# Sums placed between a product's halves, and a slot's other stages moved behind the scores

## The chip, the cores and the metric

The program runs on one core of a Trainium2 chip. Its engines are TensorE (PE, with its weight loads shown as PEld), VectorE (DVE), ScalarE (ACT), GpSimd (POOL) and SyncE (SP, which issues the DMAs). Each engine works through its own queue in order and waits at semaphores for the others. The time is the device time of one execution in microseconds; lower is better. All data are 32-bit floats.

## The reference

An encoder layer runs over a short context (2 x 77 rows of 512), and a decoder layer over 2 x 2048 rows of 512 with 16 heads of 32, a causal self-attention with relative bias, a cross-attention to the encoder's output and a feed-forward part of 2048. Cut to the decoder, where nearly all of the time is:

```python
y = tgt
yn = _ln(y, dec_n1_s, dec_n1_b)
y = y + _mha(yn, yn, dec_sa_in_w, dec_sa_in_b, dec_sa_out_w, dec_sa_out_b, sb)   # causal, biased
y = y + _mha(_ln(y, dec_n2_s, dec_n2_b), memory, dec_ca_in_w, dec_ca_in_b, dec_ca_out_w, dec_ca_out_b, cb)
h = _ln(y, dec_n3_s, dec_n3_b)
y = y + (relu(h @ dec_ff1_w.T + dec_ff1_b) @ dec_ff2_w.T + dec_ff2_b)
```

`_mha` makes q, k and v, takes `softmax(q @ k.T / sqrt(32) + bias) @ v` by heads, and multiplies by the output weights.

## The kernel before

**Blocks and units.** Self-attention comes first, up to about 1640 us. The rows are cut into eight blocks of 512 (`blocks`, two batches of four, m = 0 to 3), and a block's work into 16 units (`units`: four groups g of four heads by four tiles t of 128 rows). Unit n has 4 m + t + 1 tiles of keys, taken in pieces of up to four. The loop at L1893 goes through the pieces, up to two of a unit at a time, in this order of issue: `turn` (TensorE transposes the probabilities, ACT and DVE copy them out of PSUM), then, where the unit ends, `slot(n + 1)`, then some late exponentials (`exps`, on ACT), then scores of a unit further on (`score_two` or `score_next`; TensorE at L375, DVE takes the maxima at L384 and L391), then `values` (TensorE at L456). The scores run one to two units ahead of the turn.

**Slots.** The projections and everything else that a block needs are hung on units by hand in three lists: `light`, `jobs` and `late`. `slot(n)` (L1324) runs all of `light[n]`, then the products `jobs[n]`, then `late[n]`. `light` holds the norm of the block to come (`norm_load`, `norm_stats`, `norm_center`, and `norm_turn` with four transposes on TensorE at L305 and four copies on ACT at L310), the four steps of `spread` (reciprocals of the softmax sums on DVE, their DMAs, a multiplication on POOL), the loads of bias tiles (`load_bias`), the output's residual sums on POOL (`out_done`), the sums of tokens on POOL (`token_sums`) and weight sums for later stages (`wc_sums`, `w2_sums`, `w1_sums`). `late` holds further sums, residual loads and stores. Slot u + k of a block that begins at unit u is called slot k here; slots -5 to -1 lie in the block before.

**Products.** From the second block of a batch on, q, k, v and the output projection are made by a scheme of Strassen and Winograd's kind: a product of 512 x 512 by 512 becomes seven of half the size, numbered 1 to 7 (`PARTS`), whose results are added into the quarters "11", "12", "21", "22" of the output. `part_job` (L1108) makes one such product for k, v or the output (o): four matmuls of 256 columns in the code, two for each half f of one PSUM bank, and then sums on DVE. `pair_job` (L1032) makes two products for one half of q (a or b) with two matmuls each, in the two halves of one bank, so "a16" is products 1 and 6 of half a. `last[0]` tells a product that it is the last of its slot; `part_job` then sums each half of the bank for itself (L1150), after all of its matmuls. `todo` (L1202) puts the products on slots; the output's are at slots 6 to 9 of the next block (L1223).

**PSUM.** All matmuls write into one tile `psum` of eight banks; `bank()` (L180) hands them out in a ring, so a bank is taken again eight takings later. Semaphores between the engines are drawn from what each instruction reads and writes, in the order of the code.

**Weights.** `load_next` (L1268) is called before each product and issues the weight loads of products to come on SP, into three buffers `wqk`.

Of the kernel before, what the change touches and what calls it, by code (L numbers as in the profile page):

```python
# [12 lines left out]
ALU = mybir.AluOpType  # L13
# [41 lines left out]
def tile_encoder_decoder(ctx: ExitStack, tc: tile.TileContext, ins, out):  # L55
# [103 lines left out]
    with (  # L159
# [252 lines left out]
        def turn(pieces):  # L412

            first = units[pieces[0][0]][1] == 0
            loads = []
            for n, k0, kn in pieces:
                ks = range(k0, k0 + kn)
                if first:
                    heads = [(n, k, r) for r in range(HC) for k in ks]
                    loads += [heads[o : o + TB] for o in range(0, len(heads), TB)]  # L420
                else:
                    loads += [[(n, k, r) for r in range(HC)] for k in ks]
            for o, load in enumerate(loads):
                pt = bank()
                pts = in_turn("pts", pts_all).rearrange("p (x q) -> p x q", q=P)
                for x, (n, k, r) in enumerate(load):
                    nc.tensor.transpose(pt[:, ts(x, P)], state[n]["p"][r][:, k], ident)  # L427
                    got[n, k, r] = pts[:, x, :]
                w = len(load) * P
                free = pieces[0][0] == len(units) - 2 and (pieces[0][1] or o >= 4)  # L430
                if free or (o % 2 if first else o in (4, 6) if len(loads) == 8 else o >= (len(loads) + 1) // 2):
                    nc.vector.tensor_copy(pts[:, : len(load), :], pt[:, :w])  # L432
                else:
                    nc.scalar.copy(pts[:, : len(load), :], pt[:, :w])  # L434
# [597 lines left out]
        def pair_job(b, m, h, parts):  # L1032
# [8 lines left out]
            def run(w):  # L1041
                if parts[0] == 1:
                    for g in (2 * h, 2 * h + 1):
                        qTs[b, m, g] = sb.tile([P, MB], F32, name="q", tag="q", bufs=3)
                mm = bank()
                for j, i in enumerate(parts):
                    n = of_nT(b, m, PARTS[i][1])
                    for c in range(2):
                        nc.tensor.matmul(mm[:, ts(j, TOK)], w[:, 2 * j + c, :], n[:, c, :], start=c == 0, stop=c == 1)  # L1049
# [3 lines left out]
                got = [mm[:, ts(j, TOK)] for j in range(len(parts))]  # L1053
                if parts == (1, 6):
                    ve.tensor_scalar(d["11"], got[0], qbias[:, 2 * h : 2 * h + 1], None, ALU.add)
                    ve.tensor_tensor(d["12"], got[1], d["11"], ALU.add)
                elif parts == (7, 4):
                    ve.scalar_tensor_tensor(d["22"], got[0], qstep[:, h : h + 1], d["12"], ALU.add, ALU.add)
                    ve.tensor_tensor(d["21"], got[1], d["22"], ALU.add)
                elif parts == (2, 5):  # L1060
                    for to, j in (("11", 0), ("12", 1), ("22", 1)):
                        ve.tensor_tensor(d[to], got[j], d[to], ALU.add)
                else:
                    assert parts == (3,)
                    ve.tensor_tensor(d["12"], got[0], d["12"], ALU.add)

            return load, run, True
        n_tiles, last = {}, [False]
        PARTS = {
# [3 lines left out]
        ADDS = {2: ("11",), 3: ("12",), 5: ("22", "12")}  # L1073
# [34 lines left out]
        def part_job(kind, b, m, i):  # L1108
# [20 lines left out]
            def run(w):  # L1129
                n, mm = of_o(b, m, by) if kind == "o" else of_nT(b, m, by), bank()  # L1130
                left, right = (w, n) if kind == "k" else (n, w)
                for f in range(2):
# [4 lines left out]
                got = mm.rearrange("p (f n) -> p f n", f=2)  # L1137
                d = {to: place(to) for to in ("11", "12", "21", "22")}
                if i == 1 and kind == "k":
                    for f in range(2):  # L1140
                        nc.scalar.activation(
                            d["11"][:, f, :], got[:, f, :], AF.Identity, bias=vec("dec_sa_in_b", NC + f)
                        )
                elif i == 1:
                    nc.scalar.copy(d["11"], got)
                elif last[0] and not (i == 7 and kind == "k"):
                    for f in range(2):
                        for to in {6: ("12",), 7: ("22",), 4: ("21",)}.get(i) or ADDS[i]:
                            onto = {6: "11", 7: "12", 4: "22"}.get(i, to)
                            ve.tensor_tensor(d[to][:, f, :], got[:, f, :], d[onto][:, f, :], ALU.add)  # L1150
                elif i == 6:
                    ve.tensor_tensor(d["12"], got, d["11"], ALU.add)
                elif i == 7 and kind == "k":
                    for f in range(2):
                        ve.scalar_tensor_tensor(
                            d["22"][:, f, :], got[:, f, :], kstep[:, f : f + 1], d["12"][:, f, :], ALU.add, ALU.add
                        )
                elif i == 7:
                    ve.tensor_tensor(d["22"], got, d["12"], ALU.add)
                elif i == 4:  # L1160
                    ve.tensor_tensor(d["21"], got, d["22"], ALU.add)
                else:
                    for to in ADDS[i]:
                        ve.tensor_tensor(d[to], got, d[to], ALU.add)
# [20 lines left out]
        late = {n: [] for n in light}  # L1185

        for x, (b, m) in enumerate(blocks):
# [13 lines left out]
            else:  # L1201
                todo = {  # L1202
                    -5: "a16 a74", -4: "k1 k6", -3: "k7 k4", -2: "k2 a25", -1: "k5 k3 a3", 0: "v1 v6", 1: "v7 v4 v2",
                    2: "v5 v3", 3: "b16", 4: "b74 b25", 5: "b3",
                } if x % NMB > 1 else {
                    -4: "k1 a16 k6", -3: "a74 k7", -2: "k4 k2 a25", -1: "k5 k3 a3", 0: "v1 v6", 1: "v7 v4 v2",
                    2: "v5 v3", 3: "b16", 4: "b74 b25", 5: "b3",
# [116 lines left out]
        def slot(n):  # L1324
            for f in light[n]:
                f()
            for k, (_, run, _) in enumerate(jobs[n]):
# [3 lines left out]
                ran[0] += 1  # L1331
            for f in late[n]:
                f()
# [132 lines left out]
        for c, k in enumerate((0, 2, 4, 10)):  # L1466
            light[u + k + 2].append(lambda c=c: w2_store(c, 1))
# [425 lines left out]
        while i < len(stream):  # L1893
# [7 lines left out]
            turn(pair)  # L1901
# [7 lines left out]
            if ends and n + 1 < end:  # L1909
# [84 lines left out]
```

## Time and profile before

| what | value |
|---|---|
| median of 3 runs | 2726.84 us (2726.21 to 2733.03) |
| profiled execution: time | 2728.59 us |
| profiled execution: span, first to last instruction | 2726.8 us |
| granted TensorE clock, mean | 0.997 |
| self-attention, from the first turn to the last one's begin | 27.6 to 1641.3 us |
| cross-attention and feed-forward | 1641.3 to 2726.8 us |

The profile gives, for each group of instructions, its line, engine and operation, the tile that it writes and those that it reads, the shapes, the count, then the busy time in us and the mean of one in ns, and behind the second bar the idle time of the engine just before, with what ended it. A matmul of the code that takes 32-bit floats appears as two records. In the timeline the columns are start and length in us, then the instruction, the count of like ones merged into the row, and in brackets the idle time before it and its releaser. The ends of matmuls are modelled, so starts are the safer measure.

### The profile page before, as it was taken

Reading aid. Unit: us, or ns where it says so; the run is one execution under the profiler, and the core shown is the slowest. Engines: PE = TensorE matmul, PEld = TensorE weight load, DVE = VectorE, ACT = ScalarE, POOL = GpSimd, SP = SyncE. Lnnn points to the kernel's source line nnn. Section 1 sums busy time; section 2 is a strip of 40 time slices with the busy share of each in tenths; the row PEclk is TensorE's granted clock in tenths of the full one; section 3 lists DMA queues with packets and bytes.
Section 4 is the critical chain, followed back from the end, with each engine's and each line's share of the span. In section 5 each row is a group of like instructions: output and inputs, shape, how many; then the busy total and the mean of one; then the engine's idle time right before and its main releaser. Section 6 shows DMA issues by size and latency. Waiting matters only on the chain.

```text
span 2726.8 us, 68267 instructions
## 1 busy us (share of the span) xinstructions
PE 2708.1 (99%) x26606; PEld 2217.9 (81%) x26606; DVE 1839.9 (67%) x5445; ACT 1537.0 (56%) x2978; POOL 1002.4 (37%) x844
## 2 busy tenths in 40 slices
PE   9999999999999999999999999999999999999998
PEld 6678877777876677777777777898989898989898
DVE  4776688888885677788888783646464746464645
ACT  3554567777786547667777784444444444444431
POOL 2612235500300513322300203455556565656456
PEclk9999999999999999999999999999999999999999
DMA  8724355511213522343311206565657565656465
GB/s 242 213 92 135 126 155 164 168 50 43 67 45 89 143 76 72 111 133 98 126 50 35 79 19 220 171 214 173 213 171 239 168 216 170 218 166 219 151 224 185
DMA packets 296277, 385.10 MB, mean 141 GB/s; under 512 B 41184, under 2 KB 165648, under 8 KB 295826
## 3 DMA queue, kind: packets, MB, share of 16 engines
q1 hardware_dynamic: 295954, 380.73, 44.1%
q8 instruction: 211, 3.46, 0.5%
q14 instruction: 112, 0.92, 0.1%
HBM read 334.15 MB, written 46.47 MB: 140 GB/s over the span
## 4 chain that ended last, share of the span: by engine, by line
PE 95%; DVE 1%; ACT 1%; DMA 1%; POOL 1%; issue 1%; SPq 0%; DVEq 0%; POOLq 0%; ACTq 0%
PE psum L427 18%; PE psum L1638 14%; PE psum L1667 13%; PE psum L375 11%; PE psum L456 9%; PE psum L1134 8%; PE psum L1801 3%; PE psum L1758 3%; PE psum L1049 3%; PE psum L866 2%; PE psum L836 1%; PE psum L874 1%; PE psum L590 1%; PE psum L811 1%; PE psum L239 1%; PE psum L215 1%
## 5 line engine op out<-in xcount | busy, mean ns | idle before, releaser
L406 ACT ACTIVATE pp<-pp,nm 128x128 f32<-128x128 f32 (+15 forms) x512 | 611.8, 1200 | 28.6 <-DVE nm L401 27.8
L384 DVE TENSOR_SCALAR_CACHE_REDUCE pp<-psum 128x512 f32<-128x512 f32 (+3 forms) x1024 | 556.2, 591 | 51.3 <-PE psum L375 49.7
L434 ACT COPY pts<-psum 128x512 f32<-128x512 f32 x714 | 384.1, 594 | 312.6 <-PE psum L427 265.6
L427 PE MATMUL psum<-ident,pp 128*128 128x128 f32 x4352 | 530.4, 277 | 4.7 <-ACT nT L310 4.0
L427 PEld LDWEIGHTS psum<-ident,pp 128*128 128x128 f32 x4352 | 474.0, 141 | 55.7 <-DVE pp L384 21.4
L375 PE MATMUL psum<-kT,q 32*128 32x512 f32 (+3 forms) x2560 | 336.5, 559 | 2.5 <-DVE q L217 1.0
L456 PEld LDWEIGHTS psum<-pts,vv 128*32 128x32 f32 x8704 | 226.4, 110 | 127.4 <-DVE pp L384 55.4
L1667 PE MATMUL psum<-pp 128*128 128x128 f32 x2560 | 304.5, 276 | 1.9 <-POOL pp L962 1.6
L1667 PEld LDWEIGHTS psum<-pp 128*128 128x128 f32 x2560 | 296.3, 192 | 8.6 <-issue 2.8
L432 DVE COPY pts<-psum 128x512 f32<-128x512 f32 x374 | 245.2, 685 | 82.6 <-PE psum L427 80.3
L456 PE MATMUL psum<-pts,vv 128*32 128x128 f32 x8704 | 279.6, 276 | 0.8 <-DVE mx L391 0.3
L962 POOL TENSOR_TENSOR pp<-pp 128x512 f32<-128x512 f32 x159 | 212.8, 1356 | 111.0 <-DMA pp<-in_dec_ff_wT_dram 50.6
L1638 PE MATMUL psum<-vv,pp 128*128 128x256 f32 x1024 | 236.2, 381 | 0.0
L375 PEld LDWEIGHTS psum<-kT,q 32*128 32x128 f32 x2560 | 146.3, 183 | 107.1 <-issue 41.3
L1638 PEld LDWEIGHTS psum<-vv,pp 128*128 128x128 f32 x1024 | 190.3, 190 | 25.8 <-issue 0.5
L391 DVE CUSTOM_DVE_ANT_0 pp<-psum,bias 128x256 f32<-128x256 f32 (+1 forms) x512 | 196.0, 411 | 19.7 <-PE psum L375 19.7
L1651 DVE TENSOR_TENSOR kT<-kT,psum 128x512 f32<-128x512 f32 x96 | 65.8, 686 | 191.6 <-PE psum L1638 191.4
L1654 ACT ACTIVATE kT<-kT,vecs 128x256 f32<-128x256 f32 x192 | 86.9, 501 | 156.6 <-DVE kT L1651 155.9
L1638 PE MATMUL psum<-nT,pp 128*128 128x256 f32 x768 | 174.1, 380 | 0.5 <-DVE oT L471 0.5
L1638 PEld LDWEIGHTS psum<-nT,pp 128*128 128x128 f32 x768 | 144.2, 190 | 20.8 <-issue 1.4
L1675 ACT COPY oT<-psum 128x128 f32<-128x128 f32 x56 | 15.0, 268 | 238.9 <-PE psum L1667 238.9
L494 POOL TENSOR_TENSOR oT<-rirows,oT 128x512 f32<-128x512 f32 x30 | 38.4, 1280 | 293.6 <-DMA rirows<-rec 181.7
(272 smaller groups left out, 4110.6 us busy)
## 6 DMA issues: line engine op xcount, KB each, us to landing
pp<-w_d SPq DMA_DIRECT2D x520, 256.0 KB
pp<-in_dec_ff_wT_dram SPq DMA_DIRECT2D x112, 256.0 KB
bias<-tzg SPq DMA_DIRECT2D x128, 128.0 KB
pp<-wo_d SPq DMA_DIRECT2D x56, 256.0 KB
wqk<-in_dec_sa_in_wT_dram SPq DMA_DIRECT2D x52, 256.0 KB
wqk<-sa_q SPq DMA_DIRECT2D x84, 128.0 KB
vv<-in_enc_ff_wT_dram SPq DMA_DIRECT2D x8, 1024.0 KB
xr<-in_x_dram SPq DMA_DIRECT2D x32, 256.0 KB
```

The lines of the kernel that those rows point to most:

```text
L375: nc.tensor.matmul(banks[r][:, : kn * P], q[rows4(r), ts(t, P)], kT[rows4(r), g, k0 * P : (k0 + kn) * P], start=True, stop=True,)
L384: nc.vector.tensor_scalar(p[:, k0 : k0 + far], s[:, :far], 1.0, None, ALU.mult, ALU.max, accum_out=st["mx"][:, r, c : c + 1],)
L391: nc.vector.tensor_tensor_reduce(p[:, k0 + far : i + 1], s[:, far:kn], near[:, 2 - (kn - far) :], 1.0, LOWEST, ALU.add, ALU.max, accum_out ...
L406: nc.scalar.activation(p, p, AF.Exp, bias=nm, accum_out=to)
L427: nc.tensor.transpose(pt[:, ts(x, P)], state[n]["p"][r][:, k], ident)
L432: nc.vector.tensor_copy(pts[:, : len(load), :], pt[:, :w])
L434: nc.scalar.copy(pts[:, : len(load), :], pt[:, :w])
L456: nc.tensor.matmul(ot[rows4(r)], vv[:, k, ts(g * HC + r, HD)], got.pop((n, k, r)), start=k == k0 and (whole or not begun), stop=k == k1 - ...
L962: engine.tensor_tensor(out, a, b, ALU.subtract)
L1134: nc.tensor.matmul(mm[:, ts(f, TOK)], left[:, c, ts(f, P)], right[:, c, :], start=c == 0, stop=c == 1,)
L1638: nc.tensor.matmul(mm[:, ts(f, TOK)], a[:, c, ts(f, P)], b[:, c, :], start=fresh and f == 0 and c == 0, stop=c == 1, skip_group_check=True,)
L1667: nc.tensor.matmul(psum[:, bank_i, ts(col, P)], lhs[:, c, :], w[:, c, :], start=fresh and k in (0, 3) and c == 0, stop=c == 3, skip_group_ ...
```

## The change

Four things change.

1. In `pair_job` each of the two products is summed as soon as its two matmuls are issued, ahead of the matmuls of the second. In `part_job` a slot's last product (all but product 1) sums the first half of its bank ahead of the second half's matmuls; k's product 7, which was summed by halves behind all matmuls, now does so only as last of its slot. Others are summed behind all matmuls, as before.
2. Pairs 25 become 52, so that product 5, which is added to two quarters, comes first; "k2 a25" becomes "a52 k2"; the output's products 2 and 5 change places. Product 5's two additions change their order.
3. In the units of the second block of a batch and later, and after units 9 and 10, only the slot's products stay behind the turn. What is in `light` and `late` is issued behind the scores, ahead of the values. One list of stores (`w2_store` of the second part) moves to a list `ahead`, which runs before the products.
4. `turn` is told whether it is followed by such a slot without products (`direct`), and then gives other copies to DVE and puts its late exponential two copies before the end.

```diff
-        def turn(pieces):
+        def turn(pieces, direct):
...
-                w = len(load) * P
+                w, half = len(load) * P, len(loads) // 2
                 free = pieces[0][0] == len(units) - 2 and (pieces[0][1] or o >= 4)
-                if free or (o % 2 if first else o in (4, 6) if len(loads) == 8 else o >= (len(loads) + 1) // 2):
+                if free or (o % 2 if first else o >= half and (len(loads) - o) % 2 if direct else o in (4, 6) if len(loads) == 8 else o >= (len(loads) + 1) // 2):
...
-                if not first and o == (7 if len(loads) == 8 else min(3, len(loads) - 1)):
+                if not first and o == (max(0, len(loads) - 2) if direct else 7 if len(loads) == 8 else min(3, len(loads) - 1)):
                     exps(1)
...
-                for j, i in enumerate(parts):
-                    n = of_nT(b, m, PARTS[i][1])
-                    for c in range(2):
-                        nc.tensor.matmul(mm[:, ts(j, TOK)], w[:, 2 * j + c, :], n[:, c, :], start=c == 0, stop=c == 1)
...
-                elif parts == (2, 5):
-                    for to, j in (("11", 0), ("12", 1), ("22", 1)):
-                        ve.tensor_tensor(d[to], got[j], d[to], ALU.add)
...
+                for j, i in enumerate(parts):
+                    n, got = of_nT(b, m, PARTS[i][1]), mm[:, ts(j, TOK)]
+                    for c in range(2):
+                        nc.tensor.matmul(got, w[:, 2 * j + c, :], n[:, c, :], start=c == 0, stop=c == 1)
+                    if i == 1:
+                        ve.tensor_scalar(d["11"], got, qbias[:, 2 * h : 2 * h + 1], None, ALU.add)
+                    elif i == 7:
+                        ve.scalar_tensor_tensor(d["22"], got, qstep[:, h : h + 1], d["12"], ALU.add, ALU.add)
+                    else:
+                        for to, onto in SUMS[i]:
+                            ve.tensor_tensor(d[to], got, d[onto], ALU.add)
...
+        SUMS = {
+            2: (("11", "11"),), 3: (("12", "12"),), 4: (("21", "22"),), 5: (("12", "12"), ("22", "22")),
+            6: (("12", "11"),), 7: (("22", "12"),),
+        }
...
+                def sums(f):
...
+                    elif i == 7 and kind == "k":
+                        for x in range(2)[f]:
+                            ve.scalar_tensor_tensor(
+                                d["22"][:, x, :], got[:, x, :], kstep[:, x : x + 1], d["12"][:, x, :], ALU.add, ALU.add
+                            )
+                    else:
+                        for to, onto in SUMS[i]:
+                            ve.tensor_tensor(d[to][:, f], got[:, f], d[onto][:, f], ALU.add)
+
+                halves = last[0] and i != 1
                 for f in range(2):
                     for c in range(2):
                         nc.tensor.matmul(
                             mm[:, ts(f, TOK)], left[:, c, ts(f, P)], right[:, c, :], start=c == 0, stop=c == 1,
                         )
...
+                    if halves:
+                        sums(slice(f, f + 1))
+                if not halves:
+                    sums(slice(0, 2))
...
-                    -5: "a16 a74", -4: "k1 k6", -3: "k7 k4", -2: "k2 a25", -1: "k5 k3 a3", 0: "v1 v6", 1: "v7 v4 v2",
-                    2: "v5 v3", 3: "b16", 4: "b74 b25", 5: "b3",
+                    -5: "a16 a74", -4: "k1 k6", -3: "k7 k4", -2: "a52 k2", -1: "k5 k3 a3", 0: "v1 v6", 1: "v7 v4 v2",
+                    2: "v5 v3", 3: "b16", 4: "b74 b52", 5: "b3",
...
-                    for k, part in ((0, 1), (0, 6), (1, 7), (1, 4), (2, 2), (2, 5), (3, 3)):
+                    for k, part in ((0, 1), (0, 6), (1, 7), (1, 4), (2, 5), (2, 2), (3, 3)):
...
+        def products(n):
+            for f in ahead[n]:
+                f()
             for k, (_, run, _) in enumerate(jobs[n]):
                 load_next()
                 last[0] = k == len(jobs[n]) - 1
                 run(loaded[ran[0]])
                 ran[0] += 1
+
+        def slot(n):
+            for f in light[n]:
+                f()
+            products(n)
             for f in late[n]:
                 f()
...
-            light[u + k + 2].append(lambda c=c: w2_store(c, 1))
+            ahead[u + k + 2].append(lambda c=c: w2_store(c, 1))
...
-            turn(pair)
+            parted = ends and n + 1 < end and (units[n][1] > 0 or n in (9, 10))
+            turn(pair, parted and not jobs[n + 1])
...
-            if ends and n + 1 < end:
+            if parted:
+                products(n + 1)
+            elif ends and n + 1 < end:
                 slot(n + 1)
...
+            if parted:
+                for f in light[n + 1] + late[n + 1]:
+                    f()
             if third and not ends:
                 exps(1)
             values(pair)
```

More of the change, by code (lines that the diff above doesn't have):

```diff
@@ L1052, in run @@
                 }
[L1053 to L1059, printed above, removed]
-                elif parts == (2, 5):
-                    for to, j in (("11", 0), ("12", 1), ("22", 1)):
[L1062 to L1065, printed above, removed]
+                for j, i in enumerate(parts):
[9 more added lines that the diff above has]
+                            ve.tensor_tensor(d[to], got, d[onto], ALU.add)
             return load, run, True
         n_tiles, last = {}, [False]
+        SUMS = {
+            2: (("11", "11"),), 3: (("12", "12"),), 4: (("21", "22"),), 5: (("12", "12"), ("22", "22")),
+            6: (("12", "11"),), 7: (("22", "12"),),
+        }
         PARTS = {
@@ L1131, in run @@
                 left, right = (w, n) if kind == "k" else (n, w)
+                got = mm.rearrange("p (f n) -> p f n", f=2)
+                d = {to: place(to) for to in ("11", "12", "21", "22")}
+                def sums(f):
+                    if i == 1 and kind == "k":
+                        for x in range(2)[f]:
+                            bi = vec("dec_sa_in_b", NC + x)
+                            nc.scalar.activation(d["11"][:, x, :], got[:, x, :], AF.Identity, bias=bi)
+                    elif i == 1:
+                        nc.scalar.copy(d["11"][:, f], got[:, f])
+                    elif i == 7 and kind == "k":
+                        for x in range(2)[f]:
+                            ve.scalar_tensor_tensor(
[5 more added lines that the diff above has]
+                halves = last[0] and i != 1
                 for f in range(2):
@@ L1136, in run @@
                         )
[L1137 to L1164, printed above, removed]
+                    if halves:
+                        sums(slice(f, f + 1))
+                if not halves:
+                    sums(slice(0, 2))
             return load, run, True
@@ L1184, in tile_encoder_decoder @@
         light = {n: [] for n in range(-1, len(units) + NU)}
-        late = {n: [] for n in light}
+        late, ahead = {n: [] for n in light}, {n: [] for n in light}
         for x, (b, m) in enumerate(blocks):
@@ L1202, in tile_encoder_decoder @@
                 todo = {
[L1203 to L1204 removed]
+                    -5: "a16 a74", -4: "k1 k6", -3: "k7 k4", -2: "a52 k2", -1: "k5 k3 a3", 0: "v1 v6", 1: "v7 v4 v2",
+                    2: "v5 v3", 3: "b16", 4: "b74 b52", 5: "b3",
                 } if x % NMB > 1 else {
[L1206 to L1207 removed]
+                    -4: "k1 a16 k6", -3: "a74 k7", -2: "k4 a52 k2", -1: "k5 k3 a3", 0: "v1 v6", 1: "v7 v4 v2",
+                    2: "v5 v3", 3: "b16", 4: "b74 b52", 5: "b3",
                 }
@@ L1323, in tile_encoder_decoder @@
         light[6].append(lambda: make_bias(2, rel, v))
-        def slot(n):
-            for f in light[n]:
+        def products(n):
+            for f in ahead[n]:
                 f()
```

1 line of the change is left out of this document (removed).

## The prediction

> **What bounds the kernel now.** I read the page first (busy shares, then the chain that ended last), then the stretches of the blocks, then one slot of the timeline, then TensorE's waits.
>
> ```profile
> span 2726.8 us, 68267 instructions
> PE 2708.1 (99%) x26606; PEld 2217.9 (81%) x26606; DVE 1839.9 (67%) x5445; ACT 1537.0 (56%) x2978; POOL 1002.4 (37%) x844
> ...
> PE 95%; DVE 1%; ACT 1%; DMA 1%; POOL 1%; issue 1%; SPq 0%; DVEq 0%; POOLq 0%; ACTq 0%
> ```
>
> TensorE is busy 99% of the span and carries 95% of the chain, so whatever delays TensorE delays the end, and what shortens another engine gains only the little that TensorE waits for it.
>
> ```profile
> 369.57:589.55 219.98, 219.88 (x2658) 171.41 (x2657) 182.38 (x625) 160.15 (x276) 84.84 (x71) 1.00 0.48 144
> ...
> 1641.31:2726.80 1085.49, 1077.72 (x8408) 975.02 (x8404) 587.66 (x1128) 434.67 (x925) 596.43 (x505) 1.00 0.60 194
> ```
>
> These are the third block of the first batch and everything after attention, which the change does not touch. Columns: length, then busy time of PE, PEld, DVE, ACT, POOL, the granted clock, the DMA. In the block DVE is busy 182.38 of 219.98 us (83%) and TensorE all of it. So all that can move lies before 1641 us, and there the other engines have room while TensorE has none.
>
> One slot of the fourth block, with the products o7 and o4 (the code's four matmuls show as eight records of a product; x16 is both):
>
> ```profile
> 702.63 3.62 PE L1134 MATMUL psum<-wqk,oT 128*128 128x256 f32 x16
> ...
> 706.17 0.74 PEld L375 LDWEIGHTS psum<-kT,q 32*128 32x128 f32 x14 [0.33 <-issue]
> 706.18 1.88 PE L375 MATMUL psum<-kT,q 32*128 32x256 f32 x16
> 706.34 0.76 DVE L1150 TENSOR_TENSOR wbig<-psum,wbig 128x256 f32<-128x256 f32 x2 [1.02 <-PE psum L1134]
> ...
> 707.15 0.29 PEld L375 LDWEIGHTS psum<-kT,q 32*128 32x128 f32 x2 [0.23 <-DVE wbig L1150]
> ```
>
> The records start (3.62 - 0.38) / 15 = 0.216 us apart (0.38 is the mean of one in the rows below). o4's last starts at 705.87 and its first half's last at 702.63 + 11 x 0.216 = 705.01. L1150 here is already split into two 256-column sums, and the first reads only the first half. It starts at 706.34, 0.47 after the last record of the whole product, though DVE had been idle since 705.32 and the first half alone would have let it start at 705.48. So a read of one half of a bank is held until what was issued before it into the other half is done: the order between engines is kept by bank, not by column. This is the row that the forecast hangs on.
>
> **The change part by part.** (1) *Sums between the halves.* The code issues the first half's matmuls, its sum, then the second half's matmuls, into the same bank. If order is kept by bank, the second half's first matmul waits for the sum. How often: six blocks take the split products, each with the pairs 16, 74, 52 for two halves a and b (6) and, as a slot's last product, k6, k4 or k7, k2, v6, v2, v3 (6): 72. The output product of seven blocks has o6, o4, o2, o3 as last ones: 28. Together 100; in 12 of them (the pairs 52) the first half is summed twice. Durations:
>
> ```profile
> L1134 PE MATMUL psum<-wqk,oT 128*128 128x256 f32 x280 | 65.3, 380 | 0.0
> ...
> L1150 DVE TENSOR_TENSOR wbig<-psum,wbig 128x256 f32<-128x256 f32 x70 | 25.8, 418 | 29.3 <-PE psum L1134 20.9 <-ACT wbig L1145 6.6 <-ACT kT L867 1.0
> ...
> L1062 DVE TENSOR_TENSOR q<-psum,q 128x256 f32<-128x256 f32 x36 | 13.0, 418 | 10.5 <-PE psum L1049 10.5
> ...
> L1055 DVE TENSOR_SCALAR q<-psum,qbias 128x256 f32<-128x256 f32 x12 | 5.8, 483 | 11.4 <-PE psum L1049 11.4
> ```
>
> One stop of TensorE: 0.47 from the half's last record to the sum's start, 0.42 for the sum, 0.05 from its end to TensorE's next (L1150 ended at 707.10, the weight load of L375 began at 707.15), less the 0.216 after which the record would have started anyway: 0.72 us. Queued behind the waiting matmul are the rest of the product, the scores and the values, all that TensorE has. Sum: 88 x 0.72 = 63.4; 12 x (0.72 + 13.0/36) = 13.0; the pairs 16 and 74 start with a longer sum (L1055 483 ns; I take the same for L1058), 24 x 0.06 = 1.4: 77.8 us.
>
> That holds where DVE is free when the half is ready, which is 4 x 0.216 = 0.86 us before the whole product is. Idle time of DVE before a product's first sum, waiting for TensorE: L1055 11.4 us over 12 products, L1062 10.5 over 12 (three sums each), 0.95 and 0.88 us, so DVE is mostly free; where it is late, one eviction is in front:
>
> ```profile
> L432 DVE COPY pts<-psum 128x512 f32<-128x512 f32 x374 | 245.2, 685 | 82.6 <-PE psum L427 80.3
> ```
>
> Bounds: 0, or half of the stops behind one eviction, 50 x 0.685 = 34 us. I take 6, near the low end, since the idle rows show DVE free.
>
> The trace shows only DVE waiting for TensorE inside one bank, not TensorE for DVE. So the stop is bounded by 0 and 77.8 us; I take the whole, because the one direction that is visible is kept by bank although columns are disjoint.
>
> [...]
>
> (2) *What the stops pay back.* While TensorE stands, DVE and ACT go on evicting, and the scores that follow find banks freer:
>
> ```profile
>   issue: 41.3, 136
>   DVE pts L432: 14.5, 64
>   ACT pts L434: 6.7, 40
>   DVE wbig L1150: 3.5, 7
>   ACT nT L310: 3.1, 6
> ...
>   DVE kT L1164: 2.1, 4
>   DVE q L1062: 2.0, 5
> ```
>
> This is the line of the scores, L375: idle time before its matmuls and weight loads (us, times) and what ended it. The waits that name an eviction or a sum are 14.5 + 6.7 + 3.5 + 2.1 + 2.0 = 28.8 us, of all slots. Bounds of the gain: 0 and 28.8; I take 16, as some of these slots have no stop, and a weight load's wait is not always TensorE's. The "issue" row waits for nothing and stays.
>
> (3) *Other stages after the scores.*
>
> ```profile
> PE psum L427 <- ACT nT L310: 4.0, 2, 2.2
> ...
> L282 DVE BATCH_NORM_STATS2 bnst<-xt 128x6 f32<-128x512 f32 x28 | 19.0, 677 | 4.5 <-DMA xt<-in_x_dram 4.5
> ...
> L482 DVE RECIPROCAL ri<-sums 128x16 f32<-128x16 f32 x30 | 7.3, 242 | 0.0
> ```
>
> DVE work such as a norm's statistics (0.68 us) or a reciprocal (0.24) leaves its place in front of the sums, and the normalised tile's four ACT evictions theirs. Gain: the waits that name nT, 4.0 at the transposes and 3.1 at the scores, 7.1 at most. Against it, the norm's transposes now take a bank that the scores have just used; in the slot above the wait for a bank was 0.23. At four a block, six blocks: 24 x 0.23 = 5.5 at most. I take 7.1 less the middle of 0 to 5.5, a gain of 4.
>
> What hides the rest of the move: the bias, residual, norm and reciprocal DMAs now stand on SP behind the weight loads, which wait long for a buffer, and POOL's token sums start later.
>
> ```profile
> SPq L1118 <- PE psum L1134: 343.1, 56, 15.8
> ...
> 506.92 1.27 POOL L962 TENSOR_TENSOR xr<-nT,xt 128x512 f32<-128x512 f32 x1
> ...
> 513.39 1.89 PE L1049 MATMUL psum<-xr,wqk 128*128 128x256 f32 x8
> ```
>
> A bias is loaded two slots before the scores that read it (a slot is 219.98/16 = 13.7 us), so 15.8 us on SP fit into 27. The last token sum ends at 508.19 and pair 74 reads it from 514.25: 6 us of cover, against a shift by the scores now in front (that slot has no products), 1.88 us in the slot of the timeline. Without the cover each us of shift beyond it would cost 1 us in each of six blocks. I put 0.
>
> (4) *Evictions of a turn without products behind it* (13 turns): one copy moves between DVE (685 ns) and ACT, the job order 25 to 52 adds nothing but the double sum counted above: 0, at most 13 x 0.685 = 9 either way.
>
> Sum: 77.8 + 6 - 16 - 4 = +63.8, and 2 us off for slots whose stop overlaps a wait counted in neither row: +62. The profiled execution took 2728.59 us, 1.8 more than its span; the median of the runs is 2726.84, so its level is used: **2788 us**.
>
> **The rivals.** *TensorE does not wait* (the order is kept by columns for its writes, so the sums really run beside the second half): then only gains are left, the waits that name sums and nT, 3.5 + 2.1 + 2.0 + 7.1 = 14.7 at most; with 12 of it 2715 us. It decides from the first product on. Against it stands the row at 706.34; for it, that the two halves share no column. Chance 0.12, three quarters of it faster, the rest within the bound.
>
> *The stops are swallowed*: all named score waits and the "issue" idle of 41.3 go too: 77.8 + 6 - 28.8 - 41.3 - 7.1 = +7, 2734 us. For it, DVE's 83% in these blocks leaves evictions close to the pace of TensorE; against it, "issue" waits for no engine. Chance 0.08, half of it within the bound.
>
> *DVE is late at each stop* (its last copy of the turn stands in front of the sum): the upper bound of 34 in place of 6, and a payback of 10 for 16: +96, 2823 us. For it, o = 6 of a turn's eight copies is DVE's and ends near the first half; against it the idle rows. Chance 0.10.
>
> **How the numbers follow.** The forecast has 0.70, with its own range of 2765 to 2808. A measurement of this kernel can tell about 0.3%, 8.2 us, from no change. Faster: 0.09. Within: 0.03 + 0.04 = 0.07. Slower: 0.70 + 0.10 + 0.04 = 0.84. The range goes down to 2738, leaving the first rival and half of the second out (0.16), and up to 2823: **2738 to 2823**.
>
> **What would show it.** Right: the first sum of a split product starts 0.47 us after its fourth record; TensorE waits at L1134 and L1049 for DVE some 100 times, 0.5 us or more each, where before it waits there for nothing; TensorE's busy time stays near 2708 while the span grows; the L375 waits on L432 and L1150 shrink; L427 <- ACT nT is gone; all after attention still takes 1085 us. Wrong: matmuls of the second half that start 0.216 after the first half's last, with the sum running beside them; or score waits that shrink as much as the products grow.

## The result, and the profile after

| what | before | after |
|---|---|---|
| median of the runs side by side | 2726.76 us (4 runs) | 2839.16 us (4 runs, 2837.45 to 2845.75) |
| ratio, with its 95% interval | 1 | 1.0411 (1.0389 to 1.0434) |
| profiled execution: span | 2726.8 us | 2835.7 us |
| granted TensorE clock, mean | 0.997 | 0.993 |

The kernel became slower by 112 us, 108.9 us in the two profiled spans. The forecast had the direction and the mechanism, with +62 us, and the time lies above the range. The page of the kernel after, its busy shares, and then the stretches that answer to those shown of before (the third block, then all after attention; columns as there):

```profile
span 2835.7 us, 68334 instructions
...
PE 2723.7 (96%) x26606; PEld 2199.6 (78%) x26606; DVE 1842.4 (65%) x5437; ACT 1540.3 (54%) x2985; POOL 1000.5 (35%) x844
```

```profile
389.10:625.90 236.80, 224.11 (x2658) 169.44 (x2657) 183.38 (x623) 160.13 (x276) 93.36 (x78) 1.00 0.46 136
1750.10:2835.70 1085.60, 1077.79 (x8409) 974.99 (x8404) 587.57 (x1128) 434.45 (x925) 595.57 (x505) 1.00 0.62 194
```

As many instructions of TensorE, but it stands still 4% of a longer span. All after attention takes 1085.6 us, as before; the whole loss lies in the blocks. The third block grew from 219.98 to 236.80 us, while DVE and ACT have the same 183 and 160 us of work in it: TensorE waits.

The waits of TensorE at the lines of products (L1052 in `pair_job`, L1151 in `part_job`), in us, times, longest. Before, this view had no wait for a sum at these two functions' lines:

```profile
PE psum L1151 <- DVE wbig L1146: 21.6, 28, 3.8
PE psum L1151 <- DVE vv L1146: 20.5, 18, 3.4
PE psum L1052 <- DVE q L1059: 14.0, 12, 2.0
PE psum L1151 <- DVE kT L1146: 8.9, 16, 0.6
PE psum L1052 <- issue: 7.4, 6, 4.1
PE psum L1052 <- DVE q L1056: 4.9, 6, 1.1
PE psum L1052 <- DVE q L1054: 3.8, 6, 0.7
PE psum L215 <- DMA wqk<-in_dec_sa_in_wT_dram: 3.3, 1, 3.3
PE psum L1052 <- POOL xt L962: 3.0, 1, 3.0
```

And the slot that the forecast read, o7 and o4 in the fourth block, in the timeline of the kernel after:

```profile
743.86 2.76 PE L1151 MATMUL psum<-wqk,oT 128*128 128x256 f32 x12
...
746.71 0.42 DVE L1146 TENSOR_TENSOR wbig<-psum,wbig 128x256 f32<-128x256 f32 x1 [0.16 <-PE psum L1151]
747.18 0.73 PEld L1151 LDWEIGHTS psum<-wqk,oT 128*128 128x128 f32 x4 [0.97 <-DVE wbig L1146]
747.19 1.13 PE L1151 MATMUL psum<-wqk,oT 128*128 128x256 f32 x4 [0.57 <-DVE wbig L1146]
...
748.35 0.42 DVE L1146 TENSOR_TENSOR wbig<-psum,wbig 128x256 f32<-128x256 f32 x1 [1.22 <-PE psum L1151]
```

The twelve records are o7 and o4's first half; the twelfth starts at 743.86 + 11 x 0.216 = 746.24. The first half's sum starts 0.47 us later, at 746.71, takes 0.42, and TensorE goes on at 747.19: 0.95 us after the record before, 0.73 more than the usual step of 0.216. That is the stop of the forecast, term by term. The four records behind it span 1.13 us, where four of them take 1.03 elsewhere; that tenth recurs below.

Over all 100 split products the gap between the fourth and the fifth record of the trace, less 0.216, sums to 105.5 us (the steps of this sum are all in the timeline, like the one above). 67 of the 100 are within 0.1 us of the price that the forecast gave them. The others are longer, and they carry the surplus of 27.6 us over the 77.8 us forecast. Two of the three longest stops have their reasons in the next rows, around products o6 and v6 (timeline of the kernel after):

```profile
950.54 1.50 ACT L814 ACTIVATE pp<-psum,vecs 128x128 f32<-128x128 f32 x4
951.91 0.60 ACT L1138 COPY wbig<-psum 128x512 f32<-128x512 f32 x1
952.60 0.42 DVE L1146 TENSOR_TENSOR wbig<-psum,wbig 128x256 f32<-128x256 f32 x1 [4.63 <-ACT wbig L1138]
953.08 2.08 PE L1151 MATMUL psum<-wqk,xr 128*128 128x256 f32 x4 [3.85 <-DVE wbig L1146]
...
1051.17 2.00 ACT L867 COPY kT<-psum 77x512 f32<-77x512 f32 x4
1053.07 1.24 ACT L849 ACTIVATE pp<-pp 128x1232 f32<-128x1232 f32 x1
1054.20 0.58 ACT L1138 COPY vv<-psum 128x512 f32<-128x512 f32 x1
1054.81 0.42 DVE L1146 TENSOR_TENSOR vv<-psum,vv 128x256 f32<-128x256 f32 x1 [5.33 <-ACT vv L1138]
1055.29 2.07 PE L1151 MATMUL psum<-wqk,xt 128*128 128x256 f32 x4 [3.44 <-DVE vv L1146]
```

Product 6's first sum adds onto the quarter "11", which product 1 fills by a copy on ACT (L1138). ACT has exponentials and copies of the cross-attention in front of it, so DVE waits for ACT, and now TensorE waits for DVE. In the kernel before this same wait stood in the row of L1150 (6.6 us for "ACT wbig L1145"), where nobody waited for DVE.

### The profile page after: what moved, and what is told of

It is laid out like the page before. It is cut to its first block, busy times and chain, and to the rows that moved or that the text cites. A ratio compares the mean times of both kernels' runs of the same rounds, so it can differ in the third digit from the quotient of the medians.

```text
span 2835.7 us, 68334 instructions
## 1 busy us (share of the span) xinstructions
PE 2723.7 (96%) x26606; PEld 2199.6 (78%) x26606; DVE 1842.4 (65%) x5437; ACT 1540.3 (54%) x2985; POOL 1000.5 (35%) x844
## 4 chain that ended last, share of the span: by engine, by line
PE 49%; DVE 1%; POOL 1%; issue 1%; ACT 1%; DVEq 0%; POOLq 0%; ACTq 0%
PE psum L1636 14%; PE psum L1665 12%; PE psum L427 5%; PE psum L1799 3%; PE psum L1756 3%; PE psum L375 3%; PE psum L456 2%; PE psum L866 2%; PE psum L1151 2%; PE psum L836 1%; PE psum L874 1%; PE psum L811 1%; DVE pp L384 1%; PE psum L251 0%; ACT pp L406 0%
## 5 line engine op out<-in xcount | busy, mean ns | idle before, releaser
L427 PE MATMUL psum<-ident,pp 128*128 128x128 f32 x4352 | 530.1, 276 | 4.1 <-DVE oT L471 1.8
L427 PEld LDWEIGHTS psum<-ident,pp 128*128 128x128 f32 x4352 | 471.0, 140 | 57.6 <-issue 23.7
L375 PE MATMUL psum<-kT,q 32*128 32x512 f32 (+3 forms) x2560 | 311.6, 562 | 2.8 <-ACT kT L231 1.4
L375 PEld LDWEIGHTS psum<-kT,q 32*128 32x128 f32 x2560 | 136.6, 185 | 93.6 <-issue 47.0
```

Source lines behind the costliest of these rows:

```text
L375: nc.tensor.matmul(banks[r][:, : kn * P], q[rows4(r), ts(t, P)], kT[rows4(r), g, k0 * P : (k0 + kn) * P], start=True, stop=True,)
```

## The experiments

Two theories were set against each other from the start: that TensorE's stops at the split products are nearly the whole loss (A), and that the moved stages are a large part of it, by late token sums of GpSimd and late weight loads (B).

**Sums behind all matmuls again, all else as after.**

```diff
                 for j, i in enumerate(parts):
                     ...
                         nc.tensor.matmul(got, ...)
+                for j, i in enumerate(parts):
+                    got = mm[:, ts(j, TOK)]
                     if i == 1:
...
-                    if halves:
-                        sums(slice(f, f + 1))
-                if not halves:
+                if halves and not (i == 7 and kind == "k"):
+                    sums(slice(0, 1))
+                    sums(slice(1, 2))
+                else:
                     sums(slice(0, 2))
```

> The changed kernel with every sum of a product put back behind all its matmuls; the moved stages, the moved stores, the order 5 before 2 and the other turns of copies stay. Theory A (TensorE stops at the second half of each split product because that half writes the bank that the first half's sum reads; the stops are 105 of the 109 us): the stops go, and what stays is the moved stages: 2720 us, 2710 to 2735; the gap between a split product's fourth and fifth matmul falls from 0.93 us and more to 0.22. Rival B (the moved stages cost most of it, through late token sums of GpSimd and late weight loads): 2780 or more. Rival C (the extra work of VectorE): between 2740 and 2780, with VectorE the releaser of the matmuls behind.

Measured: 2735.23 us, 1.0028 of before (1.0018 to 1.0037). The stops are gone and 104 of the 112 us with them. What the moved stages leave, with the new order of products and the new turns, is a loss of some 7 us, not the gain that theory A had in its middle; the time lies 0.2 us above theory A's range. Its longest waits are the two that rival B named:

```profile
PE psum L215 <- DMA wqk<-in_dec_sa_in_wT_dram: 3.3, 1, 3.3
PE psum L1052 <- POOL xt L962: 3.1, 1, 3.1
```

**Sums between the halves, slots as before.** `parted` is set to False and the `w2_store` list is put back into `light`.

> Sums between halves and the order 5 before 2 alone; the slots' other stages, the stores and the copies' engines as in the kernel before. Theory A: 100 stops of some 0.72 us and the long ones at product 6, without the late token sums of slot 91: before + 95 to + 115, so 2822 to 2842 us. Rival B: within 20 us of the kernel before, 2727 to 2747.

Measured: 2840.88 us, 1.0411 (1.0397 to 1.0425), the ratio of the whole change. Its stops sum to 109.6 us. The place of the sums (with products 5 and 2 in the new order) makes the loss alone; with the stops there, the moved stages are worth nothing either way. B falls as an account of the loss.

**The halves in two banks, all else as after.**

```diff
-                mm = bank()
+                mms = [bank() for _ in parts]
...
-                    n, got = of_nT(b, m, PARTS[i][1]), mm[:, ts(j, TOK)]
+                    n, got = of_nT(b, m, PARTS[i][1]), mms[j][:, :TOK]
...
+                mms = [mm, bank() if halves else mm]
...
-                            mm[:, ts(f, TOK)], left[:, c, ts(f, P)], right[:, c, :], start=c == 0, stop=c == 1,
+                            mms[f][:, ts(f, TOK)], left[:, c, ts(f, P)], right[:, c, :], start=c == 0, stop=c == 1,
```

> The changed kernel with the two halves of each split product in two PSUM banks (a second call for a bank); everything else stays, the sums are as many and stand where they stood. Theory A (the wait is for the bank): the stops go though the sums stay between the halves; 2715 us, 2700 to 2735. Rival D (the wait is for VectorE itself or for the order of instructions, not for the bank): 2830 to 2845, the stops stay. Rival E (banks run out: 100 more banks asked for make later work wait for a bank): the stops go and other waits come, 2740 to 2780.

Measured: 2726.71 us, 0.9995 (0.9986 to 1.0004). The same slot in its timeline, with as many sums at the same places of the code:

```profile
698.62 3.62 PE L1153 MATMUL psum<-wqk,oT 128*128 128x256 f32 x16
...
701.47 0.42 DVE L1149 TENSOR_TENSOR wbig<-psum,wbig 128x256 f32<-128x256 f32 x1 [0.16 <-PE psum L1153]
...
702.35 0.42 DVE L1149 TENSOR_TENSOR wbig<-psum,wbig 128x256 f32<-128x256 f32 x1 [0.45 <-PE psum L1153]
```

o4's eight records now run through (the sixteen span 3.62 us again), and the first sum runs beside the second half: it starts 0.47 us after the half's last record, 698.62 + 11 x 0.216 = 701.00. Of the 100 stops 98 are zero, and the two that are left belong to slot 91, where GpSimd's token sums are late. So the wait is for the bank, not for VectorE and not for the order of the code.

**Product 1 of v and o copied by VectorE.**

```diff
                     elif i == 1:
-                        nc.scalar.copy(d["11"][:, f], got[:, f])
+                        ve.tensor_copy(d["11"][:, f], got[:, f])
```

> The changed kernel with product 1 of v and of o copied by VectorE instead of ScalarE; the k product's stays. Theory A: the stops of product 6 of v and o, which sum to 11.6 and 8.7 us in 12 places because its first sum waits for ScalarE's copy of product 1, fall to some 0.75 to 1.0 us each, 9 to 11 us less, and the half clock behind two of them goes, some 4 us more: 2826 us, 2818 to 2833. Rival F (VectorE is late instead: 12 more copies of 0.7 us ahead of its sums): 2836 to 2848.

Measured: 2825.88 us, 1.0362 (1.0344 to 1.0381), 13.3 us less than after, as theory A had it. The stops of o6 and v6 sum to 5.1 + 5.1 us in place of 8.7 + 11.6. o6 of the slot shown above:

```profile
949.76 0.69 DVE L1138 COPY wbig<-psum 128x512 f32<-128x512 f32 x1 [0.52 <-PE psum L1151]
950.61 0.42 DVE L1146 TENSOR_TENSOR wbig<-psum,wbig 128x256 f32<-128x256 f32 x1 [0.16 <-PE psum L1151]
951.09 1.13 PE L1151 MATMUL psum<-wqk,xr 128*128 128x256 f32 x4 [0.57 <-DVE wbig L1146]
```

A wait of 3.85 us for ACT became the plain stop. VectorE did not come late by the copy.

**Fifty more stops.** `halves = last[0] and i != 1` becomes `halves = i != 1`.

> The changed kernel with every product of k, v and o but product 1 split, not only the last of its slot: 50 more stops, 31 behind one sum and 19 behind product 5's two. Theory A: 31 x 0.72 + 19 x 1.03 = 42 us more: 2881 us, 2872 to 2895. Rival K (part is paid back, because work behind a stop finds its input ready): 2855 to 2872. Rival L (VectorE falls behind with the sums cut in two, and the stops grow): over 2895.

Measured: 2893.96 us, 1.061 (1.0596 to 1.0625): 54.8 us more than after, inside the range and 13 above its middle. The 50 new stops sum to 58.0 us by their gaps, the old ones to 99.1. Some new stops are longer than their price, where VectorE is late (one k5 5.4 us, two v5 2.6). And one reason of the lateness shows: where product 5 is not split, its two sums of 512 columns stand in front of the next product's first sum. With product 5 split, the stops of o2 behind it fall from 7.4 to 5.0 us and those of v3 from 7.5 to 4.3, each to its plain price.

**Two banks with the slots of before.** The two-bank edit, and `parted` False.

> Sums between the halves, the halves in two banks, and all stages in the slots of the kernel before. Theory A (the sums between the halves are worth some 9 us once the bank does not stop TensorE, as between the two runs with moved stages, 2735.2 and 2726.7, and the moved stages cost some 7 us): 2718 us, 2711 to 2724. Rival H (the sums' gain hangs on the moved stages, because only there the scores come straight behind the products): 2724 to 2732.

Measured: 2720.83 us, 0.9981 (0.9972 to 0.9991): by the ratio 5 us, by the medians 7 us better than the kernel before, inside theory A's range.

**Two banks with all sums behind the matmuls** (moved stages kept), which was meant to part that gain into its two possible reasons.

> The run with two banks and all moved stages, with every sum put back behind all matmuls. It parts the gain of the run with two banks over the run with the sums behind (2726.7 against 2735.2 us) into place of the sums and number of banks. Theory P (the sums that start earlier free VectorE, and the scores behind the products wait less): 2735 us, 2730 to 2739. Rival Q (more banks alone): 2724 to 2729.

Measured: 2725.87 us, 0.9992 (0.9983 to 1.0000), the same as with the sums between the halves, and inside rival Q's range. But the run does not part the two reasons. The edit moves the sums in the code and not in time, as the slot shown before has it in this run (timeline):

```profile
702.00 3.62 PE L1155 MATMUL psum<-wqk,oT 128*128 128x256 f32 x16
...
704.85 0.42 DVE L1151 TENSOR_TENSOR wbig<-psum,wbig 128x256 f32<-128x256 f32 x1 [0.16 <-PE psum L1155]
...
705.72 0.42 DVE L1151 TENSOR_TENSOR wbig<-psum,wbig 128x256 f32<-128x256 f32 x1 [0.45 <-PE psum L1155]
```

And with the sums behind in one bank:

```profile
706.38 3.62 PE L1153 MATMUL psum<-wqk,oT 128*128 128x256 f32 x16
...
710.09 0.76 DVE L1148 TENSOR_TENSOR wbig<-psum,wbig 128x256 f32<-128x256 f32 x2 [1.02 <-PE psum L1153]
```

With two banks o4's first sum starts 2.85 us after the first record, wherever the code has it (704.85 - 702.00 here, 701.47 - 698.62 with the sums between the halves); with one bank it starts 3.71 us after it. VectorE works through its own queue, the order of its sums is the same, and the sum of a half that has its own bank waits for the matmuls of that half alone. So the second bank also makes the sums early. The 9 us between the run with the sums behind and this one can come from the early sums (theory P's mechanism) or from the banks of the ring (rival Q's); no run here holds the sums back with two banks, and it stays open. The reason that the expectation for the run with old slots gave for its 9 us is as open. Where the gain with two banks sits is seen in part in the scores' line, in what ended the idle time before L375, here in the run with two banks and old slots:

```profile
  issue: 31.7, 107
```

9.6 us less than the 41.3 of the kernel before. Between the two runs with the sums behind it goes from 41.0 us with one bank to 33.2 with two. Why "issue", which names no releaser, shrinks there stays open.

**Where the moved stages cost.** Three runs put slots back. Slots 19, 67 and 91, by adding `n not in (18, 66, 90)` to `parted`, once with two banks and once with the sums behind; then eight slots:

> The run with two banks, with the slots 19, 67 and 91 not parted: their other stages go back ahead of and behind the products. Theory I (the moved stages cost at few places only: the stretches of units 66, 90 and 18, which in the run with two banks were 6.6, 4.1 and 1.8 us longer than in the kernel before, for a weight load 3.4 us late and token sums 3.2 us late): 2715 us, 2708 to 2721. Rival J (the loads and token sums are late elsewhere instead): 2722 to 2730.

> The run with all sums behind the matmuls, with the slots 19, 67 and 91 not parted. Theory I: the units 66, 90 and 18, 6.4, 3.5 and 2.3 us longer there than in the kernel before, come back: 2723 us, 2717 to 2729, at or under the kernel before. Rival J: 2731 to 2738.

> The run with two banks, with eight slots not parted: 19, 39, 55, 64, 67, 87, 91 and 103. Theory M (unit 66 stayed 5.4 us longer with slots 19, 67 and 91 put back, because slot 64's transfers, moved behind the scores, start 5 us later against the products and the weights of slot 67 land behind them): unit 66 gets back to 9.6 us or little more, and 38, 54, 86 and 102, 0.9 to 1.3 us longer each, come back too: 2714 us, 2708 to 2720. Rival N (the weights of slot 67 are bound by the bytes in front of them, wherever these are issued): 2720 to 2727, unit 66 at 14 us or more.

Measured: 2724.07 us, 0.9982 (0.9973 to 0.9991); 2729.44 us, 1.0002 (0.9994 to 1.0011), both above theory I's range, and the first inside rival J's: unit 90 came back (with two banks from 4.1 us over the kernel before to 0.6 under it), unit 66 stayed 5.4 us too long and unit 18 some 1.5 us, so theory I had the wrong slots for two of its three places. With eight slots back 2714.49 us, 0.9954 (0.9942 to 0.9966), and unit 66 as long as in the kernel before. Units 38, 54, 86 and 102 stayed 0.8 to 1.1 us too long, against the expectation; their own slots are not the reason. Unit 66 shows how such a reason is found. Three slots back, the transfers of slot 64 on SP's queue, and two products of slots 66 and 67 on TensorE (timeline):

```profile
849.19 2.67 SPq L487 DMA_DIRECT2D rec<-rt  x4
...
861.68 3.60 PE L239 MATMUL psum<-wbig,nT 128*128 128x512 f32 x8
868.87 5.21 PE L215 MATMUL psum<-nT,wqk 128*128 128x512 f32 x8 [3.59 <-DMA wqk<-in_dec_sa_in_wT_dram]
```

Eight slots back, slot 64 among them:

```profile
843.96 2.67 SPq L487 DMA_DIRECT2D rec<-rt  x4
...
861.87 3.60 PE L239 MATMUL psum<-wbig,nT 128*128 128x512 f32 x8
865.31 3.60 PE L215 MATMUL psum<-nT,wqk 128*128 128x512 f32 x8
```

The products of L239 come within 0.2 us of each other in both. With slot 64 parted its transfers begin 5.2 us later, and the weights of L215, which are queued behind them, land 3.6 us late. So it was not slot 67, where the wait shows, but slot 64, three units earlier, whose move caused it. For unit 66 theory M holds and rival N falls. Unit 18 is alike: it stays 1.5 us too long with slot 18 parted and slot 19 put back, and is as short as in the kernel before in the last run below, where slot 18 is put back too.

**Only seven slots parted**, with two banks:

> Two banks, and only the slots 11, 18, 23, 58, 82, 85 and 90 parted, whose stretches were 0.8 to 3.0 us shorter with the moved stages than with two banks alone. Theory M: the run with two banks and old slots less 2.2 + 0.8 + 1.0 + 1.4 + 1.3 + 2.5 + 2.1 = 11 us: 2710 us, 2705 to 2717. Rival N (the gains are given back at the next stretch, as a transfer or a sum arrives when it arrives): 2717 to 2724.

Measured: 2724.7 us, 0.9989 (0.998 to 0.9998), above theory M's range. My edit left the stores in `ahead`; in slots that are not parted they come behind the next sums into the same tiles, so this kernel computes the feed-forward part with other weights' sums, and units 34 and 36 became 8.0 and 5.8 us longer. The time is not that of the kernel meant, and says nothing on theory M or rival N. With the stores where the kernel before has them, and slots 10, 11, 23, 58, 82, 85 and 90 parted:

> Two banks, only the slots 10, 11, 23, 58, 82, 85 and 90 parted, and the stores of the feed-forward weights' sums where the kernel before has them (in the run with seven slots parted they came behind the next sums into the same tiles, so other weights were stored there, and units 34 and 36 grew by 8.0 and 5.8 us). Theory M: those 14 us go from 2724.7 us and the gains of units 11, 22, 57, 81, 84 and 89 stay: 2711 us, 2706 to 2717, under the run with eight slots back or level with it. Rival N (the gains are given back): 2717 to 2724.

Measured: 2710.35 us, 0.9941 (0.9927 to 0.9954). It is the fastest of all, 16 us under the kernel before, within 1 us of theory M; rival N falls. Of the 16 us the run with two banks and old slots has 5 to 7; the others come with the seven slots that stay parted.

## Why the prediction was wrong

**What held.** TensorE bounds the kernel, and the loss lies in the blocks (1085.49 and 1085.6 us behind them). The order is kept by bank: this was taken from one row of the other direction, VectorE waiting for TensorE, and the run with two banks shows it for TensorE waiting for VectorE: 98 of the 100 stops are zero there. The count of 100 is exact. The price of a plain stop, 0.72 us, is what o4 shows (0.73), and 67 stops have their own price within 0.1. The matmul of o4 behind a reader at other columns of its bank starts 0.95 us after the record before it, in place of 0.216.

**What failed: the terms around the plain stop.** The account of the two profiled spans:

| term | forecast, us | measured, us | from |
|---|---|---|---|
| plain stops | 77.8 | 77.8 | 100 stops, taken at the forecast's price, which 67 meet within 0.1 |
| stops that last longer | 6 | 27.6 | 105.5 less 77.8 |
| slow restart behind a stop | 0 | 10 | about 0.10 at each of 100 |
| half clock inside products | 0 | 6.3 | eight products in slots 70 to 91, beyond their restart |
| payback at the scores | -16 | -13.5 | idle before L375's weight loads, 107.1 to 93.6, not all of it TensorE's |
| moved stages, and 2 off | -6 | about +1 | rest to +108.9; half clock outside the products is in it too |

*The step that failed most is "I take 6, near the low end, since the idle rows show DVE free".* The idle rows are means, 0.95 and 0.88 us, and the half is ready 0.86 us before the whole product: so even on the mean DVE had hardly 0.1 us to spare when the half was ready. And I read them for L1055 and L1062 alone. Of the 27.6 us, 10.1 went when product 1 was copied by VectorE (shown). The row of L1150, quoted in the forecast, said that its sum waits for ACT, but I used only its duration: a wait of DVE that cost nothing before becomes TensorE's the moment TensorE waits for DVE. Another 5.5 us went with product 5's wide sums (shown, 2.3 at o2 and 3.2 at v3). The rest is seen in the trace and was not tried apart: 3.4 us at slot 76, where VectorE first does three rounds of the cross-attention's L843 to L846 (the wait of 4.1 us at L1052 that names no releaser), 2.4 at slot 91, and smaller ones. All of it is inside the bound of 0 to 34 that the forecast gave; the choice within it was wrong, and so was the rival that priced the upper end with late copies of the turn, which was not the cause.

*Cover.* "I put 0" for the shift of the token sums past their 6 us of cover. At slot 91 it did not hold (timeline of the kernel after):

```profile
1187.19 1.28 POOL L1101 TENSOR_TENSOR xr<-xr,row_dec_sa_out_b 128x512 f32<-128x512 f32 x1 [2.06 <-DMA xr<-in_x_dram]
...
1193.72 1.27 POOL L962 TENSOR_TENSOR xt<-nT,xt 128x512 f32<-128x512 f32 x1
...
1195.04 2.08 PE L1052 MATMUL psum<-xt,wqk 128*128 128x256 f32 x4 [3.03 <-POOL xt L962]
```

The late sum is not one in each of six blocks; one other late token sum, of the output at 1145.95, costs 1.75 us, and the kernel before waits for neither. GpSimd has four residual sums in front here, the first row's among them, and it had waited 2.06 us for their data. For SP's queue the forecast compared a bias' wait with two slots, and did not look at weights queued behind moved transfers; unit 66 is that. The gain of 4 for moved stages did come for the transposes (the wait of L427 for nT is gone), but alone the moved stages cost 7 us, as the run with the sums behind shows.

*Payback.* The amount was nearly right and the rows were not. I took the waits for evictions; the largest did not shrink. L375 after, from the same view:

```profile
  issue: 47.0, 149
  DVE pts L432: 14.0, 63
  ACT pts L434: 7.6, 42
```

14.5 became 14.0, 6.7 became 7.6, "issue" rose; what went are most of the waits for sums, those for nT and many small ones. Nor is TensorE's busy time "near 2708", as the forecast had it: it rose by 15.6 us, about what the slow restarts and the half clock inside products add up to (16.3).

**The rivals.** That TensorE does not wait fell with the timeline of o4, and that the stops are swallowed fell with the span, 108.9 us longer. The range was too narrow above: it ended at 2823, 16 us under the measured time, because its upper end took the late sums at their bound but left restart and clock at zero.

## What to carry to other kernels

Before a reader is put between two writers of one bank, price the round trip (here 0.95 us in place of 0.22, and 0.10 for the restart), then look for what that reader itself waits for: its harmless waits become those of the engine that is behind it. Where the sum has to run beside the matmuls, give each half its own bank. With a bank of its own the sum started when its half was ready, wherever the code had it (2.85 us after o7's first record in both orders); with one bank its place in the code decided whether TensorE waited (105.5 us of stops with the sums between the halves; with them behind, 104 of the 112 us lost came back). Before a run is said to part two reasons, look in its trace whether the edit moved what it was meant to move. When stages move past transfers, look for the late load several slots behind the move, and move only those slots whose stretch gets shorter.

## What the runs showed of the hardware

**The clock fell to half around five stops of 2.0 to 4.1 us.** Stretches of the kernel after, granted clock third from the right:

```profile
951.80:958.60 6.80, 5.52 (x42) 4.01 (x43) 1.94 (x11) 0.89 (x3) 0.22 (x1) 0.50 0.00 0
1003.00:1013.30 10.30, 7.78 (x40) 5.02 (x44) 3.81 (x13) 0.00 (x0) 0.00 (x0) 0.50 0.27 77
1026.90:1030.30 3.40, 3.04 (x8) 1.87 (x6) 0.75 (x2) 0.00 (x0) 1.96 (x2) 0.50 0.28 81
1054.20:1061.00 6.80, 5.71 (x44) 3.07 (x44) 2.45 (x7) 0.57 (x2) 0.00 (x0) 0.50 0.12 39
1194.20:1204.40 10.20, 8.68 (x30) 5.39 (x31) 3.00 (x12) 2.40 (x6) 5.68 (x5) 0.50 0.32 99
909.00:920.00 11.00, 7.68 (x32) 3.13 (x35) 3.84 (x13) 4.22 (x10) 3.11 (x4) 1.00 0.75 209
```

At half clock four records behind a stop span 2.08 us (the row at 953.08) in place of 1.13 behind a stop at full clock. The stretches come with the stops of 3.85, 4.07, 2.04, 3.44 and 3.03 us: four begin 0.9 to 1.9 us before TensorE goes on, one 0.4 us after. The stop of 3.32 us at unit 66, in the last row, left the clock at 1.00. The stretches are 3.4, 6.8 or 10.2 us long. The clock fell with a stop of 2.04 us and not with one of 3.32, so the stop's length alone did not decide it here. Nor is a stop needed: the kernel before has the clock at 0.50 for 6.8 us from 976.08 and for 3.4 us from 1112.62, and in the 10 us ahead of these TensorE idles 0.52 us at most at a time. That these stops cause the half clock was not tried apart. In the run with product 1 on VectorE, where the stops of o6 and v6 sum to 5.1 + 5.1 us in place of 8.7 + 11.6, the two stretches at them are gone too (o6's four records behind its stop span 1.13 us there, not 2.08), which speaks for it; but two others of 3.4 us come there, one of them behind the stop at unit 66, 4.07 us in that run.

**A restart cost a tenth of a microsecond here.** The first record behind a stop is followed by the next after 0.32 us and not 0.216 (1.13 us for four in the row at 747.19), at 85 of the 100 stops; at nine it is 0.29, and the other six lie in the half-clock stretches.

**A second bank for the products was worth 9 us** with the sums behind the matmuls in the code of both runs (2735.2 against 2725.9 us). It lets the first half's sum start 0.86 us earlier in the slot shown (2.85 in place of 3.71 us); whether that or the ring is the reason stays open.
